# Two-layer metaformer on one core: GpSimd's operand tiles of layer 0 are placed at different offsets modulo 64 bytes, and three constants of layer 1 are made between the layers

## The chip, the cores and the metric

The kernel runs on 1 core of a Trainium2 chip. The metric is the device time of that core in microseconds (us). The time before is the median of three runs. The profile is one further execution, taken by the hardware profiler; its time is given beside them.

## The reference, cut to what matters

The input is `x` of 2 x 96 channels x 96 x 96. Each of two layers adds a mixer and then a quantized feed-forward network (FFN):

```python
x = x + conv0(ln(x));  x = x + ffn0(ln(x))      # layer 0: selective scan over windows
x = x + conv1(ln(x));  x = x + ffn1(ln(x))      # layer 1: attention with 5x5 depthwise taps
```

The core of layer 0's mixer, for four scan directions, 192 inner channels and 16 states, is

```python
dA = exp(dt[..., None] * A)
h  = h * dA + (dt * u)[..., None] * b
y  = einsum('bkdn,bkn->bkd', h, c)
```

Before it stand a projection, a 3x3 convolution that yields one offset pair per pixel, a bilinear sampling with these offsets, and the softplus that makes `dt`. After it stand a norm, a gate (`Y * zs`), a projection and the FFN.

## The kernel before, in words

**Layer 0.** The image is cut into 32 stripes of 6 rows (576 tokens, `T`), 16 to a batch element. For each stripe there are three parts.

- `_l0_front` prepares it. TensorE projects and convolves; `sample` interpolates bilinearly with seven GpSimd instructions for each half of the channels (lines 609 to 615: `dif`, `top`, `bot`, with `xin` and the fractions `fr`); `steps` makes the step sizes and inputs with four GpSimd instructions for each of six blocks (lines 743 to 746: `e`, `r`, `dl`, `du`, with `x1` or `x2`). `dl` and `du` go to DRAM by DMA (`store`) and come back spread over the partitions (`dlr`, `dur`).
- `_l0_scan` runs 64 units of 128 partitions x 3 x 288 elements. In a unit (`unit`), TensorE spreads `b` into the PSUM tile `bp` (`spread`, line 1040, two buffers), VectorE multiplies it with `dur` (`product`, line 1044), VectorE scans along time into an `h` tile (`scan`, line 1060, `P.nh` = 6 buffers), GpSimd multiplies `h` in place with `cre`, the spread `c` (`times_c`, line 1065, four `cre` buffers), and TensorE folds the states into `y` (`states`, line 1077). ScalarE makes the decays `dA` (`decay`, line 1025).
- `_l0_back` norms, gates on GpSimd (line 921: `Y`, `zs`), projects, and runs the FFN, whose last step is a GpSimd add of an fp32 and an fp16 tile (line 867).

**Order.** The three parts are not issued as written: each operation is handed to `_Plan` with an engine, a cost and a due time. `_Plan.order` lays all of layer 0 out on a model of the engines with a limited number of slots for each tag, and `_Plan.issue` emits the operations in the order of their planned starts; `_in_order` then pins that order on every engine and on the DMA queue of SyncE. The front of stripe n+1 and the back of stripe n-1 are so mixed between the units of stripe n. Each engine works strictly in its order.

**Placing.** Each slot becomes a tile of its own in a pool (`issue`: `t.pool.tile(...)`). All fp32 row tiles that GpSimd reads are multiples of 64 bytes long (576 x 4 = 2304 = 36 x 64; `h`: 864 x 4 = 3456 = 54 x 64), and in the built program they all start at a multiple of 64 bytes. Only `xin`, with rows of 98 elements read from the second column on, is entered at other offsets.

**Layer 1** (`_layer1`) follows: norm and projections (`_l1_before`), attention, and rows (`_l1_rows`). The constants `k.ones`, `k.join` and `k.onesb` are used there alone; `tile_metaformer` makes them ahead of layer 0, with two GpSimd memsets and two VectorE copies.

Of the kernel before, what the change touches and what calls it, by code (L numbers as in the profile page):

```python
# [1 line left out]

# [6 lines left out]
F32 = mybir.dt.float32  # L9
HP = mybir.dt.float16  # L10
BF = mybir.dt.bfloat16
# [14 lines left out]
C = 96  # L26
HW = 96
NTOK = HW * HW
WIN = 6
NW = HW // WIN  # L30
SEQ = WIN * WIN
T = WIN * HW
H2 = T // 2
# [4 lines left out]
NBL = C // CB  # L38
# [5 lines left out]
HEADS = 3  # L44
HD = 32
# [27 lines left out]
class _Tile:  # L73


    def __init__(self, plan, pool, tag, bufs, shape, dtype, name):
        self.pool, self.tag, self.shape, self.dtype, self.name = pool, tag, shape, dtype, name
        self.slots = plan.slots.setdefault((id(pool), tag), [[None, 0.0, ""] for _ in range(bufs)])
        self.queue = plan.queues.setdefault((id(pool), tag), [])
        self.slot, self.ap, self.users, self.writes, self.reads = None, None, [], [], []  # L80

    def place(self):

        if self.tag != "p" and self.queue[0] is not self:
            return None
        return min((s for s in self.slots if s[0] is None), key=lambda s: s[1], default=None)
# [15 lines left out]
class _Plan:  # L102
# [4 lines left out]
        self.k, self.ops, self.slots, self.queues = k, [], {}, {}  # L107
        self.rate = {}

    def tile(self, pool, shape, tag, bufs=1, dtype=F32, name=None):  # L110
        return _Tile(self, pool, tag, bufs, shape, dtype, name or tag)

    def held(self, ap, name):

# [98 lines left out]
    def issue(self):  # L213
        tab = None
        for o in self.order():
            for t in o.tiles:
                if t.ap is None:
                    n = [s is t.slot for s in t.slots].index(True)
                    t.ap = t.pool.tile(
                        t.shape, t.dtype, tag=f"{t.tag}{n}", name=t.name, bufs=1  # L220
                    )
            if o.tab is not None and o.tab != tab:
                tab = o.tab
                if tab == "e":
                    _exp_ln(self.k)
            o.run()


def _exp_ln(k):

    k.nc.scalar.add_instruction(
        mybir.InstLoadActFuncSet(
            name=k.nc.get_next_instruction_name(),
            engine=mybir.EngineType.Activation,
            act_func_set_id=EXP_LN,
            ins=[],
            outs=[],
        )
    )
# [205 lines left out]
def _l0_front(k, P, S, f, x, b, s, at):  # L445
# [3 lines left out]
    nc = k.nc  # L449
# [1 line left out]
    lo, hi = max(r0, 0), min(r0 + 8, HW)  # L451
    half2 = lambda v: v.rearrange("p (c n) -> p c n", c=2)
    n0 = len(S.ops)
    temp = lambda shape, name: S.tile(P.front, shape, "g", P.ng, name=name)
    ps = lambda name: S.tile(P.ps, [128, 512], "p", P.np, name=name)
    row = lambda name, bufs, dtype=F32: S.tile(P.front, [128, T], name, bufs, dtype)

    def pe(cols, run, r, w, also=()):
        S.op("pe", _cost("pe", cols), run, r, w, also=also)

    def act(cols, run, r, w, tab=None, times=1):
        S.op("act", times * _cost("act", cols), run, r, w, tab=tab)
# [4 lines left out]
    def pool(cols, run, r, w):  # L467
        S.op("pool", _cost("pool", cols), run, r, w)
# [55 lines left out]
            project(half, c)  # L524


    zs = f.zs = S.tile(P.hand, [C, 2, T], "zs", 2)

    def gate(half, c):
        pz = ps("pz")  # L530
# [13 lines left out]
    t = temp([C, 2, T], "t")  # L544
# [25 lines left out]

    fr = temp([C, 2, WIN, HW], "fr")

    def offset(yx, c):
        po = ps("po")
# [20 lines left out]

    xs0 = f.xs0 = S.tile(P.hand, [C, 2, T], "xs0", 2)
    xs1 = S.tile(P.front, [C, 2, T], "xs1", 1)
    dif, top, bot = temp([C, 2, 7, HW], "dif"), temp([C, 2, WIN, HW], "top"), temp([C, 2, WIN, HW], "bot")  # L600
    g = nc.gpsimd
    tt = g.tensor_tensor

# [42 lines left out]
    def order_of(o, xs):  # L646
# [48 lines left out]
            (rest,), (cd,))  # L695


        x1, x2 = row("x1", 1), row("x2", 1)

        block = lambda b: xs.ap[(b % NBL) * CB : (b % NBL) * CB + CB, b // NBL]  # L700

# [12 lines left out]
        def steps(m):  # L714


            bias = k.dt_b[:, o, m : m + 1]
            u = x2 if m == 2 else x1
            e, r, w, du = row("e", 2), row("r", 2), row("dl", 2), row("du", 2)
            for c in range(2):  # L720
                def half(c=c):
                    pt = ps("pt")
                    cols = slice(c * H2, (c + 1) * H2)
                    pe(H2, lambda: nc.tensor.matmul(  # L724
                        pt.ap[:, :H2], k.w_dt[:, o, m, :], xd.ap[:, cols],
                        start=True, stop=True), ((xd, c),), (pt,), (e, r))

                    def both():
                        nc.scalar.activation(e.ap[:, cols], pt.ap[:, :H2], AF.Abs, bias=bias)
                        nc.scalar.activation(r.ap[:, cols], pt.ap[:, :H2], AF.Relu, bias=bias)  # L730

                    act(H2, both, (pt,), ((e, c), (r, c)), times=2)

                half()

            def grow():
                nc.scalar.activation(e.ap, e.ap, AF.Exp, scale=-1.0)
                nc.scalar.activation(w.ap, e.ap, AF.Identity, bias=k.one)
                nc.scalar.activation(du.ap, w.ap, AF.Identity, bias=k.less)  # L739

            act(T, grow, (), (e, w, du), tab="e", times=3)
            act(T, lambda: nc.scalar.activation(w.ap, w.ap, AF.Ln), (), (w,), tab="e")
            pool(T, lambda: tt(e.ap, e.ap, du.ap, ALU.subtract), (du,), (e,))  # L743
            pool(T, lambda: tt(r.ap, r.ap, e.ap, ALU.add), (e,), (r,))
            pool(T, lambda: tt(w.ap, w.ap, r.ap, ALU.add), (r,), (w,))
            pool(T, lambda: tt(du.ap, w.ap, u.ap, ALU.mult), (w, u), (du,))  # L746


            def past():
                if m < 2:  # L750
                    g.memset(w.ap[:, (SEQ - 1 if m else 0) :: SEQ], PAST)
                else:
                    g.memset(w.ap[0:64, 0::SEQ], PAST)
                    g.memset(w.ap[64:128, SEQ - 1 :: SEQ], PAST)

            pool(16, past, (), (w,))

            def store(src, dst):
                def run():
                    if m < 2:  # L760
                        nc.sync.dma_start(dst[m].ap[:, 0:4, :], src.ap)
                    else:
                        for kk in range(2):
                            nc.sync.dma_start(
                                dst[kk].ap[:, 4:6, :], src.ap[64 * kk : 64 * kk + 64])

                S.op("sp", 1.0, run, (src,), [(d, m) for d in (dst if m == 2 else dst[m : m + 1])])

            d = [[v[o], v[o + 2]] for v in (f.dl, f.du)]
            store(w, d[0])  # L770
            store(du, d[1])

        for m in range(3):
            steps(m)
# [217 lines left out]
def _l0_section(k, P, S, f, first, o, h, kk, py, at, tau):  # L992


    nc = k.nc
# [12 lines left out]
    for name, d in (("dlr", f.dl[kg]), ("dur", f.du[kg])):  # L1008
        t = S.tile(P.rep, [128, NBL, T], name, 2)
# [24 lines left out]
    def unit(u, i, c, cre, dA, t0):  # L1034
        toks = slice(c * H2, (c + 1) * H2)
        bp = S.tile(P.ps, [128, 1024], "bp", 2)
        ht = S.tile(P.rep, [128, NBL, H2], "h", P.nh)

        def spread():
            nc.tensor.matmul(  # L1040
# [806 lines left out]
@with_exitstack  # L1847
def tile_metaformer(ctx: ExitStack, tc: tile.TileContext, a, out):
    nc = tc.nc
    k = Ctx()  # L1850
    k.nc = nc
    const = ctx.enter_context(tc.tile_pool(name="const", bufs=1))
    k.ident = const.tile([128, 128], F32, tag="ident", name="ident")
    make_identity(nc, k.ident)

    def filled(name, shape, v):
        t = const.tile(shape, F32, tag=name, name=name)
        nc.gpsimd.memset(t, v)
        return t

    k.kvq = [const.tile([C, C], F32, tag=n, name=n) for n in ("k_w", "v_w", "q_w")]
    k.mean96 = filled("mean96", [C, C], 1.0 / C)

    k.less_mean = const.tile([C, C], F32, tag="less_mean", name="less_mean")
    nc.vector.tensor_tensor(k.less_mean, k.ident[:C, :C], k.mean96, ALU.subtract)
    k.minus_mean192 = filled("minus_mean192", [C, C], -0.5 / C)
    k.less_mean192 = const.tile([C, C], F32, tag="less_mean192", name="less_mean192")
    nc.vector.tensor_tensor(k.less_mean192, k.ident[:C, :C], k.minus_mean192, ALU.add)
    k.mean192 = filled("mean192", [C, C], 1.0 / (2 * C))
    k.ones = filled("ones", [128, C], 1.0)  # L1870

    k.join = const.tile([128, C], F32, tag="join", name="join")
    nc.vector.tensor_copy(k.join, k.ident[:, :C])
    last = slice((HEADS - 1) * HD, HEADS * HD)
    nc.vector.tensor_copy(k.join[C:, last], k.ident[C:, C:])
    k.onesb = const.tile([128, 128], BF, tag="onesb", name="onesb")
    nc.gpsimd.memset(k.onesb, 1.0)
    k.eps6 = filled("eps6", [128, 1], EPS_LNC)
    k.eps5 = filled("eps5", [128, 1], EPS)
    k.one = filled("one", [128, 1], 1.0)  # L1880
    k.less = filled("less", [128, 1], -1.0)

    scratch = ctx.enter_context(tc.tile_pool(name="x2d", bufs=1, space=DRAM))
    x2d = scratch.tile([NB, C, NTOK], F32, tag="x2d", name="x2d")
    _layer0(k, tc, a, a["x"], x2d)
    _layer1(k, tc, a, x2d, out)


# [60 lines left out]
```

## Time and profile before

| | |
|---|---|
| median of 3 runs | 8538.53 us (8529.44 to 8542.1) |
| the profiled execution's own time | 8525.04 us |
| its span | 8523.3 us |
| TensorE matmul busy | 7295.1 us (86%) |
| VectorE busy | 7815.6 us (92%) |
| ScalarE busy | 6339.3 us (74%) |
| GpSimd busy | 6026.9 us (71%) |
| first and last scan (line 1060) start | 153.5 and 6472.0 us |

The times of single instructions come from the profiled execution. In a row of a group the columns are: line, engine, operation, output and inputs by tile name, shapes, count, then the busy time in us and the mean of one instruction in ns, and last the idle time of the engine just before them with what ended it. PE is TensorE, DVE is VectorE, ACT is ScalarE, POOL is GpSimd, SP is SyncE. In a timeline a row gives start and length in us; brackets at its end give the idle time before and who ended it. A busy time is no bound by itself: GpSimd is at 71% of the span only because layer 1, about a quarter of the span, hardly uses it.

### The profile page before, as it was taken

The page shows a single profiled execution, that of the slowest core. Times are in us where ns is not written, and L with a number is a line of the kernel's source. Part 1 is how long each engine was busy: PE and PEld are TensorE (multiplying, and loading weights), DVE is VectorE, ACT ScalarE, POOL GpSimd, SP SyncE. Part 2 cuts the span into 40 slices and gives each one's busy share as a digit, 9 for nine tenths or more (in the row PEclk, how much of TensorE's full clock was granted, in tenths as well). Part 3 has the DMA queues.
Part 4 walks back from the last instruction along what each step waited for, and adds up shares of the span by engine and source line. Part 5 has one row for each costly group of instructions (what it writes and reads, how often), then busy time and mean ns, then how long its engine had stood idle before and what let it go on. Part 6 is the DMA issues. An engine that isn't in the chain of part 4 may idle for free. (4 is left out here: it accounts for less than half of the span.)

```text
span 8523.3 us, 118902 instructions
## 1 busy us (share of the span) xinstructions
PE 7295.1 (86%) x43653; PEld 3402.1 (40%) x43653; DVE 7815.6 (92%) x5398; ACT 6339.3 (74%) x10688; POOL 6026.9 (71%) x3835
## 2 busy tenths in 40 slices
PE   7888888888888888888888888888866999989998
PEld 4443444444443444444444444443423223542245
DVE  3899999999999999999999999999996998959988
ACT  5777777777777777777777777777755886778867
POOL 4999999999999999999999999999984000110001
PEclk8899999999989888988999998989867999989999
DMA  2444444444444444444444444444442000110001
GB/s 89 141 153 148 150 152 147 148 151 144 149 146 144 151 146 152 149 150 153 146 150 151 146 145 151 146 151 150 146 143 76 3 2 14 34 48 3 2 21 32
DMA packets 339992, 985.62 MB, mean 116 GB/s; under 512 B 50152, under 2 KB 51872, under 8 KB 339104
## 3 DMA queue, kind: packets, MB, share of 16 engines
q1 hardware_dynamic: 337488, 977.74, 36.8%
q8 instruction: 347, 5.69, 0.3%
q14 instruction: 253, 2.07, 0.1%
q10 hardware_dynamic: 1904, 0.12, 0.0%
HBM read 797.19 MB, written 139.25 MB: 110 GB/s over the span
## 5 line engine op out<-in xcount | busy, mean ns | idle before, releaser
L1065 POOL TENSOR_TENSOR h<-h,cre 128x864 f32<-128x864 f32 x2048 | 4121.2, 2027 | 428.2 <-DVE h L1060 277.3
L1060 DVE TENSOR_TENSOR_SCAN h<-dA,bp 128x864 f32<-128x864 f32 x2048 | 3996.6, 1953 | 105.5 <-PE y L1077 25.5
L1025 ACT ACTIVATE dA<-dlr,A 128x576 f32<-128x576 f32 x3072 | 2155.9, 765 | 815.3 <-DVE h L1060 758.5
L1044 DVE TENSOR_TENSOR bp<-dur,bp 128x864 f32<-128x864 f32 x2048 | 2135.5, 1044 | 201.8 <-PE bp L1040 80.4
L1077 PE MATMUL y<-h,fold 128*32 128x288 f32 (+2 forms) x18432 | 1856.8, 449 | 465.3 <-POOL h L1065 444.4
L551 PE MATMUL pc<-xin,off 96*96 96x288 f32 x4608 | 1331.7, 421 | 0.1
L1077 PEld LDWEIGHTS y<-h,fold 128*32 128x32 f32 x18432 | 756.1, 117 | 1245.1 <-POOL h L1065 809.6
L1413 ACT ACTIVATE pr<-sc 128x960 f32<-128x960 f32 (+1 forms) x1080 | 954.1, 937 | 201.7 <-PE sc L1409 181.5
L1040 PE MATMUL bp<-bt,selb 128*128 128x288 bf16 x2048 | 640.9, 314 | 516.9 <-DVE h L1060 506.5
L1493 DVE TENSOR_TENSOR sums<-sums,pr 128x3840 f32<-128x3840 f32 (+1 forms) x240 | 959.0, 3996 | 56.7 <-ACT pr L1413 34.4
L1585 POOL MEMSET vch<- 96x32 f32 x16 | 2.4, 153 | 1298.1 <-DVE dist L1447 1208.1
L551 PEld LDWEIGHTS pc<-xin,off 96*96 96x96 f32 x4608 | 705.9, 165 | 505.9 <-issue 236.8
L1040 PEld LDWEIGHTS <-selb 128*128 128x128 bf16 x2048 | 201.5, 99 | 1204.1 <-DVE h L1060 930.4
L1409 PE MATMUL sc<-qH,kH 32*128 32x480 f32 (+1 forms) x3240 | 627.1, 602 | 10.1 <-DMA q<-qH 5.1
L1409 PE MATMUL sc<-q,kH 32*128 32x480 f32 (+1 forms) x1080 | 564.6, 602 | 0.0
L1475 PE MATMUL av<-pr,vT 128*32 128x480 f32 (+1 forms) x4320 | 533.2, 564 | 3.7 <-ACT av L1500 3.5
L1666 DVE SCALAR_TENSOR_TENSOR acc<-vch,lepe_w,acc 96x1152 f32<-96x1152 f32 x320 | 469.2, 1466 | 8.2 <-ACT vch L1601 0.4
L867 POOL TENSOR_TENSOR x<-x,fy 96x576 f32<-96x576 f32 x32 | 55.0, 1719 | 479.5 <-ACT fy L866 415.4
L1409 PEld LDWEIGHTS sc<-qH,kH 32*128 32x128 f32 x3240 | 218.9, 184 | 419.1 <-issue 219.9
L724 PE MATMUL pt<-xd,w_dt 96*128 96x288 f32 x768 | 290.5, 474 | 15.1 <-ACT xin L516 7.2
L743 POOL TENSOR_TENSOR e<-e,du 128x576 f32<-128x576 f32 x192 | 272.6, 1420 | 31.4 <-ACT du L739 30.9
L746 POOL TENSOR_TENSOR du<-dl,x 128x576 f32<-128x576 f32 x192 | 271.5, 1414 | 6.6
(270 smaller groups left out, 10018.1 us busy)
## 6 DMA issues: line engine op xcount, KB each, us to landing
cre<-c_d SPq DMA_DIRECT2D x1024, 288.0 KB
dur<-du_d SPq DMA_DIRECT2D x256, 864.0 KB
dlr<-dl_d SPq DMA_DIRECT2D x256, 864.0 KB
x<-xs SPq DMA_DIRECT2D x512, 72.0 KB
du_d<-du SPq DMA_DIRECT2D x128, 288.0 KB
dl_d<-dl SPq DMA_DIRECT2D x128, 288.0 KB
du_d<-du SPq DMA_DIRECT2D x128, 144.0 KB
dl_d<-dl SPq DMA_DIRECT2D x128, 144.0 KB
```

The costliest lines, as they stand in the source:

```text
L551: pe(H2, lambda: nc.tensor.matmul(pc.ap[:C, :H2], k.w_c1[:, ih, tap, oh * C : (oh + 1) * C], xin.ap[:, ih, 3 * c + dy : 3 * c + dy + 3, dx ...
L1025: nc.scalar.activation(dA.ap[:, :, blk, :], dlr.ap[:, blk, :].rearrange("p (c n) -> p c n", c=2), AF.Exp, scale=k.A[:, i, kg, h, blk : blk ...
L1040: nc.tensor.matmul(bp.ap[:, :H2], k.selb[:, kk, i, :], f.bc[o].ap[:, toks], start=True, stop=True)
L1044: nc.vector.tensor_tensor(bp.ap[:, : NBL * H2].rearrange("p (b n) -> p b n", b=NBL)[:, ::-1], dur.ap[:, ::-1, toks], bp.ap[:, :H2].unsquee ...
L1060: nc.vector.tensor_tensor_scan(hv, dv, bv, 0.0, ALU.mult, ALU.add)
L1065: nc.gpsimd.tensor_tensor(ht.ap, ht.ap, cre.ap[:, toks].unsqueeze(1).to_broadcast([128, NBL, H2]), ALU.mult)
L1077: nc.tensor.matmul(dst, k.fold, v, start=False, stop=stop)
L1409: nc.tensor.matmul(two[to // 2][:, to % 2, :n], kH[rows, k0 : k0 + 128], q, start=True, stop=True)
L1413: nc.scalar.activation(pr[:, 2 * i : 2 * i + 2, :n], two[i][:, :, :n], AF.Exp, scale=HD**-0.5)
L1475: nc.tensor.matmul((main if s < HEADS else other)[s * HD : (s + 1) * HD, :n], vT[:, blk, hd, :], pr[:, place(s, p), :n], start=at == 0, st ...
L1493: nc.vector.tensor_tensor(both, both, pr[:, :, :, :n], ALU.add)
L1666: S.op("dve", 1.43, lambda: nc.vector.scalar_tensor_tensor(acc.ap, src(), W.lw[:, t : t + 1], acc.ap, ALU.mult, ALU.add), (vch,), (acc,))
```

## The change

A tile may now be given a `skip`: its slot is allocated longer by `lead` elements (equal to `skip` unless given), and the tile begins `skip` elements (of 4 bytes) after the slot's start. The tiles of layer 0 that GpSimd reads in pairs get different skips. The lengths of slots change with that, so slots that follow can start elsewhere modulo 64 as well. No instruction of layer 0 is added, removed or changed in shape.

```diff
+def _place(t, tag):
+
+    if t.skip is None:
+        return t.pool.tile(t.shape, t.dtype, tag=tag, name=t.name, bufs=1)
+    n = math.prod(t.shape[1:])
+    flat = t.pool.tile([t.shape[0], n + t.lead], t.dtype, tag=tag, name=t.name, bufs=1)
+    v, d = flat[:, t.skip : t.skip + n], t.shape[1:]
...
-    zs = f.zs = S.tile(P.hand, [C, 2, T], "zs", 2)
+    zs = f.zs = S.tile(P.hand, [C, 2, T], "zs", 2, skip=12)
...
-    fr = temp([C, 2, WIN, HW], "fr")
+    fr = temp([C, 2, WIN, HW], "fr", 5)
...
-    dif, top, bot = temp([C, 2, 7, HW], "dif"), temp([C, 2, WIN, HW], "top"), temp([C, 2, WIN, HW], "bot")
+    dif, top, bot = temp([C, 2, 7, HW], "dif"), temp([C, 2, WIN, HW], "top", 2), temp([C, 2, WIN, HW], "bot")
...
-        x1, x2 = row("x1", 1), row("x2", 1)
+        x1, x2 = row("x1", 1, skip=14), row("x2", 1, skip=9)
...
-            e, r, w, du = row("e", 2), row("r", 2), row("dl", 2), row("du", 2)
+            e, du, r, w = (row(name, 2, skip=n) for name, n in (("e", 0), ("du", 1), ("r", 2), ("dl", 6)))
...
-        ht = S.tile(P.rep, [128, NBL, H2], "h", P.nh)
+        ht = S.tile(P.rep, [128, NBL, H2], "h", P.nh, skip=(2, 4, 8, 1)[i], lead=8)
```

The second part moves the three constants of layer 1 into a pool that is opened after `_layer0`; four small constants that layer 0 needs stay ahead of it.

```diff
-    k.ones = filled("ones", [128, C], 1.0)
...
     _layer0(k, tc, a, a["x"], x2d)
+    const = ctx.enter_context(tc.tile_pool(name="const1", bufs=1))
+    k.ones = const.tile([128, C], F32, tag="ones", name="ones")
+    nc.gpsimd.memset(k.ones, 1.0)
 
     k.join = const.tile([128, C], F32, tag="join", name="join")
     nc.vector.tensor_copy(k.join, k.ident[:, :C])
...
     nc.vector.tensor_copy(k.join[C:, last], k.ident[C:, C:])
     k.onesb = const.tile([128, 128], BF, tag="onesb", name="onesb")
     nc.gpsimd.memset(k.onesb, 1.0)
```

In the built programs the order of instructions on TensorE, ScalarE and SyncE is the same before and after. On GpSimd the two memsets alone change place. On VectorE the two copies into `join` move to between the layers, the second behind the first line of `band`, and a few short instructions of the weights' preparation change places with neighbours.

Modulo 64 bytes, the second operand then starts after the first by: `e`,`du` 4 or 36; `r`,`e` 56; `dl`,`r` 16 or 48; `dl`,`x1` 32; `dl`,`x2` 12; `dif`,`fr` 20; `bot`,`fr` 20; `bot`,`top` 8; `Y`,`zs` 48. An `h` slot is now 3488 bytes, which is 54 x 64 + 32, so `h` slots start at 0 and 32 in turn, and `h` and `cre` differ by 16, 24, 28, 32, 48, 56, 60 or 0, each for 256 of the 2048 units. Line 867 is left as it is.

More of the change, by code (lines that the diff above doesn't have):

```diff
@@ L1 @@
+import math
 from contextlib import ExitStack
@@ L80, in __init__ @@
         self.slot, self.ap, self.users, self.writes, self.reads = None, None, [], [], []
+        self.skip = None
     def place(self):
@@ L108, in __init__, with tile @@
         self.rate = {}
-    def tile(self, pool, shape, tag, bufs=1, dtype=F32, name=None):
-        return _Tile(self, pool, tag, bufs, shape, dtype, name or tag)
+    def tile(self, pool, shape, tag, bufs=1, dtype=F32, name=None, skip=None, lead=0):
+        t = _Tile(self, pool, tag, bufs, shape, dtype, name or tag)
+        t.skip, t.lead = skip, lead or skip
+        return t
     def held(self, ap, name):
@@ L218, in issue @@
                     n = [s is t.slot for s in t.slots].index(True)
-                    t.ap = t.pool.tile(
-                        t.shape, t.dtype, tag=f"{t.tag}{n}", name=t.name, bufs=1
-                    )
+                    t.ap = _place(t, f"{t.tag}{n}")
             if o.tab is not None and o.tab != tab:
@@ L226, in issue @@
             o.run()
+def _place(t, tag):
[4 more added lines that the diff above has]
+    v, d = flat[:, t.skip : t.skip + n], t.shape[1:]
+    names = [f"d{j}" for j in range(len(d))]
+    if len(d) == 1:
+        return v
+    return v.rearrange(f"p ({' '.join(names)}) -> p {' '.join(names)}", **dict(zip(names[1:], d[1:])))
 def _exp_ln(k):
@@ L453, in _l0_front @@
     n0 = len(S.ops)
-    temp = lambda shape, name: S.tile(P.front, shape, "g", P.ng, name=name)
+    temp = lambda shape, name, skip=0: S.tile(P.front, shape, "g", P.ng, name=name, skip=skip)
     ps = lambda name: S.tile(P.ps, [128, 512], "p", P.np, name=name)
-    row = lambda name, bufs, dtype=F32: S.tile(P.front, [128, T], name, bufs, dtype)
+    row = lambda name, bufs, dtype=F32, skip=None: S.tile(
+        P.front, [128, T], name, bufs, dtype, skip=skip)
     def pe(cols, run, r, w, also=()):
@@ L1869, in tile_metaformer @@
     k.mean192 = filled("mean192", [C, C], 1.0 / (2 * C))
-    k.ones = filled("ones", [128, C], 1.0)
[L1872 to L1877, printed above, removed]
     k.eps6 = filled("eps6", [128, 1], EPS_LNC)
@@ L1885, in tile_metaformer @@
     _layer0(k, tc, a, a["x"], x2d)
+    const = ctx.enter_context(tc.tile_pool(name="const1", bufs=1))
+    k.ones = const.tile([128, C], F32, tag="ones", name="ones")
+    nc.gpsimd.memset(k.ones, 1.0)
+    k.join = const.tile([128, C], F32, tag="join", name="join")
+    nc.vector.tensor_copy(k.join, k.ident[:, :C])
+    last = slice((HEADS - 1) * HD, HEADS * HD)
+    nc.vector.tensor_copy(k.join[C:, last], k.ident[C:, C:])
+    k.onesb = const.tile([128, 128], BF, tag="onesb", name="onesb")
+    nc.gpsimd.memset(k.onesb, 1.0)
     _layer1(k, tc, a, x2d, out)
```

## The prediction

> **What bounds the kernel now.** I read first the busy time in windows. From 3500 to 4500 us, deep in layer 0, the columns are TensorE, its weight loads, VectorE, ScalarE, GpSimd:
>
> ```profile
> 3500.00:4500.00 1000.00, 852.32 (x5046) 418.04 (x5045) 964.73 (x683) 770.45 (x1322) 934.06 (x576) 0.90 0.47 149
> ```
>
> VectorE is the bound, with 35 us in 1000 idle; GpSimd comes second, at 93%. The groups of instructions name the work:
>
> ```profile
> L1065 POOL TENSOR_TENSOR h<-h,cre 128x864 f32<-128x864 f32 x2048 | 4121.2, 2027 | 428.2 <-DVE h L1060 277.3
> L1060 DVE TENSOR_TENSOR_SCAN h<-dA,bp 128x864 f32<-128x864 f32 x2048 | 3996.6, 1953 | 105.5 <-PE y L1077 25.5
> L1044 DVE TENSOR_TENSOR bp<-dur,bp 128x864 f32<-128x864 f32 x2048 | 2135.5, 1044 | 201.8 <-PE bp L1040 80.4
> ```
>
> Undisturbed, VectorE repeats a unit every 2.945 us, as the timeline near the end of layer 0 shows:
>
> ```profile
> 6439.56 1.95 DVE L1060 TENSOR_TENSOR_SCAN h<-dA,bp 128x864 f32<-128x864 f32 x1
> 6441.42 1.04 DVE L1044 TENSOR_TENSOR bp<-dur,bp 128x864 f32<-128x864 f32 x1
> 6442.50 1.95 DVE L1060 TENSOR_TENSOR_SCAN h<-dA,bp 128x864 f32<-128x864 f32 x1
> ```
>
> A stripe's floor is 64 x 2.945 = 188.5 us, plus two each of line 508 (0.533), line 912 (0.732) and line 827 (0.431), 3.4 us: 191.9 us. From the first scan (153.5) to the last (6472.0) a stripe takes 6318.5 x 64 / 2047 = 197.5 us. So 5.6 us a stripe, about 180 us in all, are VectorE's waits: the most that quicker GpSimd work can return in mid-layer. The waits of VectorE from 200 to 6400 us say for whom (total, times, longest):
>
> ```profile
> DVE bp L1044 <- PE bp L1040: 80.4, 80, 3.3
> DVE bp L1044 <- PE y L1077: 48.9, 31, 3.1
> DVE h L1060 <- PE y L1077: 25.5, 12, 3.8
> DVE bp L1044 <- POOL h L1065: 9.9, 22, 0.8
> ```
>
> With two lesser POOL rows (3.7 and 2.7) that is 171 us. TensorE is named most, but it works in order, and the timeline of one stall shows it held up by GpSimd:
>
> ```profile
> 4196.69 1.20 PE L1077 MATMUL y<-h,fold 128*32 128x288 f32 x6 [1.99 <-POOL h L1065]
> 4198.16 5.97 POOL L1065 TENSOR_TENSOR h<-h,cre 128x864 f32<-128x864 f32 x3
> 4202.33 0.97 PE L1077 MATMUL y<-h,fold 128*32 128x216 f32 x12
> 4203.56 2.03 DVE L1044 TENSOR_TENSOR bp<-dur,bp 128x864 f32<-128x864 f32 x2 [3.33 <-PE bp L1040]
> ```
>
> GpSimd had run e, h, r, dl, h, du without a pause from 4188.4; TensorE lost 1.99 us on `h`, then had 4.3 us of the back's projection (lines 932 and 935, from 4198.0) ahead of the next `bp`. So about 60% of this stall (1.99 of 3.33) is GpSimd's and 40% is TensorE's own density.
>
> **What an offset costs on GpSimd.** The groups by form, GpSimd alone:
>
> ```profile
> L743 POOL TENSOR_TENSOR e<-e,du 128x576 f32<-128x576 f32 x192 | 272.6, 1420 | 31.4 <-ACT du L739 30.9 <-DVE bp L1044 0.4
> L613 POOL TENSOR_TENSOR bot<-bot,xin 96x576 f32<-96x576 f32 x64 | 83.6, 1306 | 2.8
> L609 POOL TENSOR_TENSOR dif<-xin 96x672 f32<-96x672 f32 x64 | 83.5, 1306 | 30.9 <-ACT xin L516 30.9
> L867 POOL TENSOR_TENSOR x<-xr,fy 96x576 f32<-96x576 f32 x32 | 40.8, 1276 | 18.2 <-ACT fy L866 18.2
> L1193 POOL TENSOR_TENSOR hs<-xn 96x288 f32<-96x288 f32 x32 | 21.2, 664 | 88.2 <-DVE xn L1171 88.2
> L1196 POOL TENSOR_TENSOR xs<-hs 96x144 f32<-96x144 f32 x32 | 15.6, 486 | 2.5
> ```
>
> Operands at equal offsets modulo 64 lie on one line: 144 elements 486 ns, 576 about 1416, 864 2027, that is 178 + 2.139 ns an element. The two groups whose operands are one element apart (lines 609 and 1193) lie on another: (1306 - 664) / (672 - 288) = 1.672 ns an element, 182 ns fixed. Line 613, at offsets that shift by 8 bytes a row from 20 to 60, lies between: (1306 - 180) / 576 = 1.955. Line 867 drifts through all offsets, fp32 against fp16: 1.90.
>
> **What the Trainium skill says.** (1) "GPSIMD Engine Reference", section "Elementwise — side-by-side cycle accounting", gives about 2.6 cycles an element for two inputs, which share one read port, and calls that the floor; the specifications say 1.2 GHz. The equal-offset line agrees (2.139 x 1.2 = 2.57); lines 609 and 1193, at 2.0, are below that floor, so here the measurement decides. (2) "SBUF — State Buffer", "Who interferes with whom": a VectorE instruction with at most one SBUF input doesn't contend with GpSimd. Product and scan each have one; the trace agrees, with scans at 1923 to 1956 ns throughout. A quicker GpSimd doesn't shorten VectorE's instructions. (3) The same page, "Operand start alignment", says that any multiple of the element size is legal, and that its runs timed nothing.[...]
>
> **The change part by part.**
> - `times_c`, 2048 instructions. Bounds: 182 + 864 x 1.672 = 1626 ns and 180 + 864 x 1.955 = 1869; 256 units keep equal offsets (2027). The new offsets are mostly like line 613's, but no row is quite like it, so I take the middle, 1748, for seven eighths: mean 1783, saving 244 ns. 64 x 0.244 = 15.6 us a stripe.
> - Lines 743 to 746, 24 a stripe: bounds 1145 and 1306, taken 1226 of 1416: 4.6 us. Lines 610, 612, 614 and 615, 8 a stripe at about 0.18: 1.4. Line 921, 2 at 0.19: 0.4. Lines 609, 611 and 613 stay apart and stay as they are.
> - Sum: GpSimd falls from 188 us a stripe (64 x 2.027 + 24 x 1.416 + 8 x 1.405 + 6 x 1.306 + 2 x 1.416 + 1.28 + memsets) to 166; 177 if all offsets are like line 613's, 154 if all are free. VectorE needs 191.9, so GpSimd's backlog after a burst of front work drains several times faster than now.
> - What VectorE gets: of the 171 us, 60% if the stall shown is typical (103), all if backlog was the root each time (in 172 of its 175 gaps over 0.15 us GpSimd had run for 6 us without a pause of 0.15 us, counted in the timeline). I take 70%: 120 us. Late next is TensorE's density.
> - The start: VectorE first waits 45.5 us for `dur`. On that path lie 8 cheaper instructions of `sample` (76.6 to 93.4 us, 1.4 us) and 8 to 12 of `steps` (114.4 to 136.0, 2 us, some under ScalarE's `du`): 3 us. After the last scan: one `h`, two `Y`: 0.6 us.
> - Other readers and writers of the moved tiles (ScalarE, TensorE, VectorE's scan, DMA): taken at nothing. TensorE's taps of line 551 read `xin` 0, 1 and 2 elements along and start 243 ns apart each; ScalarE's copies to `xin` (one element in) take a median 464 ns against 466 into aligned `axc`. Not shown is the scan's write: bounds 0 and 5% (98 ns), an estimate: three times the spread that line 1060 shows by itself, 1923 to 1956 ns. The moved DMAs (`x1`, `x2`, `dl`, `du`) ride in queues 47% busy and land ahead of need; only the first stripe's are on the path, at most 1 to 2 us. A gain there has no reason.
> - The constants: two memsets (0.18 and 0.20 us) and two copies (about 0.2 each, as line 339) leave a start where GpSimd next waits 31 us: nothing. Between the layers, GpSimd's stand before the `xs` memset (6510.75) and end well before its 10.6 us wait for `xn`; VectorE's stand in front of `band`, which waits for TensorE and ScalarE already, and 6.2 us of idle follow before `xn`. Without that cover: 0.4 us each. Layer 1's tiles move by 1024 bytes, so its offsets stay.
>
> Sum: 120 + 3 + 0.6 = 124 us. The profiled execution, 8525.0 with 1.7 us around its span, would be 8401; its median lies 13.5 us higher, so I forecast 8415.
>
> **Rivals.**
> - TensorE's density is most of the stalls. For it: TensorE is 85% busy, with 4.3 us of matmuls in a row. Against it: 404 us of TensorE's own waits are for `h`. A third of 171 us, and 3: 8538 - 60 = 8478.
> - The offset isn't what parts lines 609 and 1193 from the rest, and `h` stays near 2027: the change doesn't do what it says. Against it: three points on one line, two on the other. About 8535.
> - Slower: the scan, on the bounding engine, writes `h` off 64 bytes and lengthens. It decides from 124 / 2048 = 61 ns (3%) on; at 5% it costs 2048 x 98 ns = 200 us: 8415 + 200 = 8615. Against it: line 1447 writes `dist` one element in, at 630 ns for 480 elements, no more an element than line 1651's 544 for 384.
>
> **How the numbers follow.** Forecast (8350 to 8465) 0.70, density 0.15, no effect 0.08, slower scan 0.07. The low end is all 180 us and the start's; the high end takes in the density case. Faster by over 0.2% (17 us, what a measurement here can tell from no change) 0.85, within it 0.08, slower 0.07.
>
> **What would show it.** Line 1065 between 1626 and 1869 ns, in up to eight steps, one near 2027; lines 743 to 746 at 1145 to 1306; 609, 613 and 867 unchanged; 1060 and 1044 within 10 ns; GpSimd near 83% in mid-layer, VectorE near 98%; TensorE's wait for `h` a fraction of 404 us. A scan over 2015 ns, or waits of VectorE that stay at 171 us, would make me wrong.

## The result, and the profile after

The changed kernel takes 8444.31 us (median of 4 runs, 8443.66 to 8449.37), against 8537.53 us (median of 4) for the kernel before: a ratio of 0.9893, with a 95% interval of 0.9881 to 0.9906. That is 93 us less; 124 were forecast. Lines have moved by 16: the product is now line 1060, the scan 1076, `times_c` 1081, the fold 1093, the spread 1056, and the four lines of `steps` 759 to 762.

The time came from where it was looked for:

| profiled execution | before | after |
|---|---|---|
| its own time (span) | 8525.0 (8523.3) | 8449.4 (8447.6) |
| start to first scan | 153.5 | 152.1 |
| first scan to last scan | 6318.5 | 6237.6 |
| of that over VectorE's floor (6132) | 186 | 105 |
| last scan to end | 2051.3 | 2057.9 |
| GpSimd a stripe (sum of its durations in layer 0, over 32) | 188.5 | 179.1 |

VectorE's floor between the two scans is worked out from the profile of before: 2047 units of 2.945 us, and 103.9 us of the three lines of the front and the back (508, 912 and 827) that fall in between.

Now the window of the changed kernel in mid-layer (columns as before: TensorE, weight loads, VectorE, ScalarE, GpSimd):

```profile
3500.00:4500.00 1000.00, 855.82 (x5102) 418.47 (x5106) 975.31 (x693) 779.04 (x1346) 907.21 (x589) 0.91 0.48 152
```

VectorE rose from 96.5% to 97.5%; GpSimd fell only from 93.4% to 90.7%. Its groups by form tell why:

```profile
L1081 POOL TENSOR_TENSOR h<-h,cre 128x864 f32<-128x864 f32 x2048 | 3965.5, 1947 | 616.1 <-DVE h L1076 357.4 <-PE pc L567 141.6 <-PE y L1093 40.1
L762 POOL TENSOR_TENSOR du<-dl,x 128x576 f32<-128x576 f32 x192 | 271.7, 1415 | 6.6
L761 POOL TENSOR_TENSOR dl<-dl,r 128x576 f32<-128x576 f32 x192 | 270.9, 1411 | 9.1 <-ACT dl L758 4.1
L760 POOL TENSOR_TENSOR r<-r,e 128x576 f32<-128x576 f32 x192 | 231.9, 1208 | 3.3
L759 POOL TENSOR_TENSOR e<-e,du 128x576 f32<-128x576 f32 x192 | 231.1, 1204 | 33.3 <-ACT du L755 33.2
L937 POOL TENSOR_TENSOR Y<-Y,zs 96x576 f32<-96x576 f32 x64 | 89.9, 1405 | 12.5 <-DVE Y L928 12.5
L629 POOL TENSOR_TENSOR bot<-bot,xin 96x576 f32<-96x576 f32 x64 | 83.5, 1305 | 2.8
L631 POOL TENSOR_TENSOR bot<-bot,fr 96x576 f32<-96x576 f32 x64 | 76.9, 1202 | 1.4
```

All these pairs now differ modulo 64, but for an eighth of `h`, and yet lines 761, 762 and 937 took what equal offsets took, while others fell by 200 ns. Within line 1081 there are only two speeds: 512 instructions took up to 1757 ns, the others 1994 or more. Its instructions, sorted by the addresses of the two tiles in the built program (second operand's start minus the first's, bytes modulo 64; 256 units each), have these means:

| difference | 0 | 16 | 24 | 28 | 32 | 48 | 56 | 60 |
|---|---|---|---|---|---|---|---|---|
| modulo 16 | 0 | 0 | 8 | 12 | 0 | 0 | 8 | 12 |
| ns | 2028 | 2025 | 1714 | 2024 | 2024 | 2021 | 1715 | 2023 |

The other pairs whose rows are plain (one run of elements, without `xin`) fit the same rule: fast at 4 or 8 modulo 16 (`e`,`du` 4 and 36; `r`,`e` 56; `fr` 20; `bot`,`top` 8), slow at 0 or 12 (`dl`,`r` 16 and 48; `dl`,`x1` 32; `dl`,`x2` 12; `Y`,`zs` 48). That is the theory tested below. The rival is that a pair need only differ modulo 64. (In the built program of before, the tiles of these pairs all start at 32 modulo 64, not at a multiple of 64 as said above. Their differences are 0 all the same.)

VectorE's waits in the changed kernel, 150 to 6400 us:

```profile
DVE bp L1060 <- PE bp L1056: 51.1, 53, 2.2
DVE bp L1060 <- PE y L1093: 28.8, 19, 3.6
DVE h L1076 <- PE y L1093: 27.2, 16, 3.6
DVE h L1076 <- POOL h L1081: 2.4, 1, 2.4
```

The first two rows fell from 129 to 80; the third didn't fall (27.2 us, before 25.5). TensorE's wait for `h` fell from 404 us to about 150. First the row of before, then two of the changed kernel, all from 200 to 6400 us:

```profile
PE y L1077 <- POOL h L1065: 404.1, 455, 3.5
```
```profile
PE bp L1056 <- DVE h L1076: 679.6, 737, 3.2
PE y L1093 <- POOL h L1081: 152.0, 156, 2.7
```

### The profile page after: what moved, and what is told of

It is laid out like the page before. It is cut to its first block, busy times and chain, and to the rows that moved or that the text cites. A ratio compares the mean times of both kernels' runs of the same rounds, so it can differ in the third digit from the quotient of the medians.

```text
span 8447.6 us, 118902 instructions
## 1 busy us (share of the span) xinstructions
PE 7320.6 (87%) x43653; PEld 3406.4 (40%) x43653; DVE 7806.9 (92%) x5398; ACT 6339.6 (75%) x10688; POOL 5742.1 (68%) x3835
## 5 line engine op out<-in xcount | busy, mean ns | idle before, releaser
L1081 POOL TENSOR_TENSOR h<-h,cre 128x864 f32<-128x864 f32 x2048 | 3965.5, 1947 | 616.1 <-DVE h L1076 357.4
L1076 DVE TENSOR_TENSOR_SCAN h<-dA,bp 128x864 f32<-128x864 f32 x2048 | 3996.8, 1953 | 105.4 <-PE y L1093 27.2
L1060 DVE TENSOR_TENSOR bp<-dur,bp 128x864 f32<-128x864 f32 x2048 | 2133.6, 1043 | 132.9 <-PE bp L1056 51.1
L761 POOL TENSOR_TENSOR dl<-dl,r 128x576 f32<-128x576 f32 x192 | 270.9, 1411 | 9.1 <-ACT dl L758 4.1
L762 POOL TENSOR_TENSOR du<-dl,x 128x576 f32<-128x576 f32 x192 | 271.7, 1415 | 6.6
```

The source lines that it names most:

```text
L1060: nc.vector.tensor_tensor(bp.ap[:, : NBL * H2].rearrange("p (b n) -> p b n", b=NBL)[:, ::-1], dur.ap[:, ::-1, toks], bp.ap[:, :H2].unsquee ...
L1076: nc.vector.tensor_tensor_scan(hv, dv, bv, 0.0, ALU.mult, ALU.add)
L1081: nc.gpsimd.tensor_tensor(ht.ap, ht.ap, cre.ap[:, toks].unsqueeze(1).to_broadcast([128, NBL, H2]), ALU.mult)
```

## The experiments

"Mid-layer waits" are the time from first to last scan less 6132 us, in the profiled execution of each run. The kernel before was timed again in each of the three rounds of experiments, with medians of 8528.6, 8531.7 and 8532.4 us. The ratios are to the kernel before of the same round, so kernels of different rounds are compared by ratio.

**Which offset is fast?** Three kernels are the changed one with another `h` line.

```diff
-        ... skip=(2, 4, 8, 1)[i], lead=8)
+        ... skip=2, lead=8)      # e1_h_skip2
+        ... skip=4, lead=8)      # e2_h_skip4
+        ... skip=3, lead=8)      # e3_h_skip3
```

Expected of the first: 

> Every h tile begins 2 elements (8 bytes) into its slot, whatever the quarter; slots still start at 0 and 32 in turn, so cre lies 56 or 24 bytes after h modulo 64. In the changed kernel the units at 56 and 24 took 1715 ns and those at 0, 16, 28, 32, 48 and 60 took 2021 to 2028. Theory (the second operand's start minus the first's, modulo 16 bytes: 4 or 8 is fast, 0 or 12 slow): all 2048 units near 1715. GpSimd then needs 64 x 0.23 = 15 us less a stripe than in the changed kernel, 165 us against VectorE's 192. If VectorE's waits are GpSimd's backlog, most of the 100 us left in mid-layer go: about 8380 to 8400. If TensorE's density holds them, 8420 to 8440.

Of the second: 

> Every h tile begins 4 elements (16 bytes) into its slot: cre lies 48 or 16 bytes after h modulo 64, never 0. If it is enough to differ modulo 64 (as the change has it), h takes clearly less than 2027 ns and the time is at or below the changed kernel's 8444. Theory (modulo 16): every unit stays near 2024, and the time goes back up, to about 8490 to 8520, as the front's cheaper instructions are all that remains.

Of the third: 

> Every h tile begins 3 elements (12 bytes) into its slot: cre lies 52 or 20 bytes after h modulo 64, 4 modulo 16. Theory (4 or 8 modulo 16 is fast): all units near 1715, time as with 2 elements. Rival (only a distance of half a 16-byte line helps h, and the mirror images 4 and 12 are alike): all units near 2024, since 12 is slow in the changed kernel (units at 28 and 60).

The row of `times_c` among GpSimd's groups, first 2, then 4, then 3 elements:

```profile
L1081 POOL TENSOR_TENSOR h<-h,cre 128x864 f32<-128x864 f32 x2048 | 3494.9, 1713 | 1057.7 <-DVE h L1076 624.7 <-PE pc L567 175.6 <-PE y L1093 103.6
```
```profile
L1081 POOL TENSOR_TENSOR h<-h,cre 128x864 f32<-128x864 f32 x2048 | 4121.0, 2024 | 499.7 <-DVE h L1076 269.3 <-PE pc L567 148.7 <-PE y L1093 21.8
```
```profile
L1081 POOL TENSOR_TENSOR h<-h,cre 128x864 f32<-128x864 f32 x2048 | 3494.8, 1713 | 1067.1 <-DVE h L1076 625.1 <-PE pc L567 168.6 <-PE y L1093 112.7
```

With 4 elements every `h` and `cre` differ modulo 64 and none is faster: the rival falls. Times: 8445.75 (ratio 0.9899, 0.9884 to 0.9914), 8472.15 (0.9934, 0.992 to 0.9948) and 8442.93 (0.9898, 0.9883 to 0.9913). The times that had been expected of the first failed: 15 us a stripe less on GpSimd than in the changed kernel returned nothing (0.9899 against 0.9893), though TensorE's wait for `h` fell further, from 152 to 97 us. In the second, `h` is as slow as before, so its 56 us came from the front and `zs`, more than the theory had given them (8490 to 8520).

**Does the sign count?** Every `h` begins 1 element in, and the operands of `times_c` are named in the other order.

```diff
-        ht = ... skip=(2, 4, 8, 1)[i], lead=8)
+        ht = ... skip=1, lead=8)
-                ht.ap, ht.ap, cre.ap[:, toks]...to_broadcast([128, NBL, H2]), ALU.mult)
+                ht.ap, cre.ap[:, toks]...to_broadcast([128, NBL, H2]), ht.ap, ALU.mult)
```

Expected: 

> As the changed kernel, but every h tile begins 1 element in and the product names cre first and h second, so the second operand starts 4 (modulo 16) after the first, where the order h, cre would give 12, slow in the changed kernel (2023 ns). Theory (the sign counts: second minus first, 4 or 8 fast): all units near 1715. Rival (the tile that is written in place decides, or where the tile lies in its line): near 2024.

```profile
L1081 POOL TENSOR_TENSOR h<-cre,h 128x864 f32<-128x864 f32 x2048 | 3498.0, 1715 | 1053.2 <-DVE h L1076 615.4 <-PE pc L567 169.9 <-PE y L1093 104.3
```

With `h` one element in, the order `h`, `cre` had given 2023 in the changed kernel (12 modulo 16 and its like, 28 and 60); the order `cre`, `h` gives 1715. Tiles one element apart are slow when the second operand starts 4 bytes before the first (12 modulo 16) and fast when it starts 4 after. This kernel was run once: 8438.31 us.

**Where does the gain come from?** Each part alone.

```diff
-        ht = ... skip=(2, 4, 8, 1)[i], lead=8)      # e6_front_only: h as before
+        ht = S.tile(P.rep, [128, NBL, H2], "h", P.nh)
```

e7_h_only keeps this line of the changed kernel and drops all other skips; e5_consts_only drops every skip and keeps the move of the constants.

Expected of the constants alone: 

> The three constants of layer 1 are made between the layers; every tile of layer 0 starts where it did before. Theory: they lie beside other work on both sides, so the time is that of the kernel before within 0.1%, about 8530. Rival: layer 1 begins later by them (the profile of the changed kernel has 6.6 us more after the last scan): 8535 to 8540, with the 6.6 us in the same place.

Of the front and `zs` alone: 

> As the changed kernel, but the h tiles start where they did before (same offset as cre modulo 64): every h unit near 2026 ns. Theory (modulo 16): it equals the kernel with h 4 elements in, 8472, since that gave h no gain either; so about 56 us of the 93 come from 20 cheaper short instructions a stripe, 4 us a stripe. Rival (the h units carry most of the gain): 8500 or more.

Of `h` alone: 

> As the changed kernel in h alone; the front's tiles and zs start where they did before. A quarter of the h units near 1715 ns, 5 us a stripe less of GpSimd. If stalls come from bursts of front work between h units, less than half of the gain: 8490 to 8510. If all GpSimd time counts alike, 5 of the 9 us a stripe saved and so about 8480.

| kernel | GpSimd a stripe, us | mid-layer waits | time | ratio to before |
|---|---|---|---|---|
| before | 188.5 | 186 | 8531.7 | |
| constants alone | 188.3 | 186 | 8532.2 | 1.0002 (0.9993 to 1.001) |
| `h` alone | 183.1 | 138 | 8490.9 | 0.996 (0.9944 to 0.9975) |
| front and `zs` alone | 184.1 | 135 | 8472.9 | 0.9938 (0.9923 to 0.9953) |
| the change | 179.1 | 105 | 8444.3 | 0.9893 (0.9881 to 0.9906) |
| `h` at 2 elements | 164.1 | 102 | 8445.8 | 0.9899 (0.9884 to 0.9914) |

The row of the change is the result above (kernel before: 8537.5 us); that of `h` at 2 elements is of the round with 8528.6. The constants cost nothing that the timed runs can tell. The front part saves 4.4 us of GpSimd a stripe and returns 59 us; `h` saves 5.4 and returns 41. The theory for the front part (8472) came true, and so did the first figure for `h` alone (8490 to 8510). But that a microsecond saved in the middle of a burst is worth more isn't shown: the two intervals overlap, and in the profiles the mid-layer waits fell almost alike, by 51 and 48 us. The front part alone, at 8472.9, equals the kernel with `h` 4 elements in, at 0.9938 and 0.9934: to move `h` without making GpSimd faster returns nothing. After 9 us a stripe the curve is flat.

**All pairs near.** The fix by the rule found:

```diff
-    zs = ... skip=12)
+    zs = ... skip=2)
-        x1, x2 = row("x1", 1, skip=14), row("x2", 1, skip=9)
+        x1, x2 = row("x1", 1, skip=1), row("x2", 1, skip=1)
-            ... (("e", 0), ("du", 1), ("r", 2), ("dl", 6)))
+            ... (("e", 0), ("du", 1), ("r", 2), ("dl", 0)))
-        ht = ... skip=(2, 4, 8, 1)[i], lead=8)
+        ht = ... skip=2, lead=8)
```

Expected: 

> All pairs of layer 0 that GpSimd reads, but those with xin, get 4 or 8 modulo 16: h 2 elements in, dl 0, x1 and x2 1, zs 2, the rest as in the changed kernel. Theory: lines of dl, du and Y fall from 1405 to 1415 to about 1205, h to 1715; GpSimd needs about 161 us a stripe. Against the kernel with h at 2 alone that is 5 us a stripe less: another 5 to 25 us if backlog still costs VectorE, nothing if TensorE's density is all that is left. 8370 to 8400 by the first, 8420 by the second.

```profile
L762 POOL TENSOR_TENSOR du<-dl,x 128x576 f32<-128x576 f32 x192 | 231.5, 1206 | 6.6
L761 POOL TENSOR_TENSOR dl<-dl,r 128x576 f32<-128x576 f32 x192 | 231.2, 1204 | 10.9 <-ACT dl L758 6.4
L937 POOL TENSOR_TENSOR Y<-Y,zs 96x576 f32<-96x576 f32 x64 | 76.8, 1201 | 10.9 <-DVE Y L928 10.9
```

The three slow lines fell as the rule has it; GpSimd needs 161.2 us a stripe. The time is 8437.09 us (0.9891, 0.9875 to 0.9906), the best of the kernels that compute everything, though its interval doesn't part it from the change, and it is above both times expected. The mid-layer waits stay at 98 us. What holds them? Its timeline shows one of the stalls that recur every second stripe:

```profile
4889.29 1.27 PE L948 MATMUL pp<-xr,ident 96*96 96x288 f32 x2 [0.92 <-ACT r L746]
4890.36 2.13 PE L951 MATMUL pp<-zs,w_outb 96*96 96x288 f32 x4
4891.13 5.06 POOL L1081 TENSOR_TENSOR h<-h,cre 128x864 f32<-128x864 f32 x3
4892.28 1.91 PE L951 MATMUL pp<-Y,out_proj 96*96 96x288 f32 x4
4894.03 0.29 PE L1056 MATMUL bp<-bt,selb 128*128 128x288 bf16 x1
4894.35 1.06 DVE L1060 TENSOR_TENSOR bp<-dur,bp 128x864 f32<-128x864 f32 x1 [1.71 <-PE bp L1056]
```

VectorE waits for `bp`, which stands behind 4.7 us of the back's projection, one operation to the plan, where a unit lasts 2.945 us. No wait for `h` is in it. The block had itself begun late, after 0.92 us in which TensorE waited for ScalarE (`r`, line 746). The next such stall, 20 us on, has no such wait ahead of its block and is longer:

```profile
4907.98 1.28 PE L948 MATMUL pp<-xr,ident 96*96 96x288 f32 x2
4914.41 2.03 DVE L1060 TENSOR_TENSOR bp<-dur,bp 128x864 f32<-128x864 f32 x2 [2.28 <-PE bp L1056]
```

**Is it TensorE's load?** Part of the convolution is left out of the kernel with all pairs near, so this one doesn't compute the whole:

```diff
-            pe(H2, lambda: nc.tensor.matmul(
+            pe(H2, lambda: None if ih and tap < 8 else nc.tensor.matmul(
```

Expected: 

> The kernel with all pairs at 4 or 8 modulo 16, with 8 of the 18 matmuls of each convolution left out (the second half's first 8 taps); the order of all else is kept. TensorE has 2048 fewer matmuls, some 500 us. Theory (TensorE's density between two bp matmuls holds VectorE now): the 97 us of VectorE's waits in mid-layer fall to under 40, and the time to 8360 to 8385. Rival (what is left is ScalarE, GpSimd bursts or the buffers of h and bp): waits stay over 75 us and the time at 8425 to 8437.

VectorE's waits from 150 to 6400 us:

```profile
DVE bp L1060 <- PE bp L1056: 57.2, 61, 4.3
DVE bp L1060 <- PE y L1093: 21.4, 25, 3.3
DVE h L1076 <- PE y L1093: 19.3, 14, 3.5
```

The time is 8430.70 us (0.9884, 0.9869 to 0.9899), and the mid-layer waits are 105. The theory, as put, fell, and the rival's figures came. The small gain isn't mid-layer's: the first scan starts at 129.6 us instead of 151.3. But the relief was smaller than expected. In the windows of mid-layer the granted clock was 0.85 to 0.87 (the third figure from the end), against 0.89 to 0.92, and a matmul of the convolution took 482 ns instead of 422, so that TensorE's busy share fell from 86% to 81% only. Without and then with these matmuls left out:

```profile
3500.00:4500.00 1000.00, 859.56 (x5115) 421.69 (x5115) 973.86 (x691) 780.64 (x1347) 817.34 (x587) 0.90 0.48 151
L567 PE MATMUL pc<-xin,off 96*96 96x288 f32 x4608 | 1335.3, 422 | 1.5 <-ACT xin L532 1.5
```
```profile
3500.00:4500.00 1000.00, 808.42 (x4794) 385.77 (x4794) 975.59 (x691) 788.38 (x1360) 822.22 (x593) 0.86 0.48 152
L567 PE MATMUL pc<-xin,off 96*96 96x288 f32 x2560 | 892.5, 482 | 1.7 <-ACT xin L532 1.4
```

So this much less load returned nothing in mid-layer. What a lighter TensorE at an unchanged clock would return isn't shown.

**Is it the block?** In the kernel with all pairs near, the two products with `zs` are left out of the projection:

```diff
-                for h in range(2):
+                for h in range(2 * n):
```

Expected: 

> The kernel with all pairs at 4 or 8 modulo 16; of the five products in a row of the back's projection (one block on TensorE of 5.3 us in its timeline, with a bp matmul behind it) the two with zs are left out, which leaves 3.2 us; order kept. Leaving out 592 us of convolution moved the time by 7 us only, but those matmuls stand singly between others. Theory (the length of a block that TensorE can't break, not its load, holds VectorE): the stalls of 1.7 and 2.3 us a pair of stripes go, VectorE's waits fall by 30 to 60 us, time 8380 to 8405. Rival (the h and bp buffers, or ScalarE): no change, 8430 to 8437.

(The 592 us in it were an estimate, 8/18 of the convolution; in the two rows above TensorE's busy time falls by 443.) The time is 8422.78 us (0.987, 0.9854 to 0.9887). That is 14 us below the kernel with all pairs near, or 18 by the ratios, whose intervals still overlap. The mid-layer waits are 82. VectorE's waits from 150 to 6400 us:

```profile
DVE bp L1060 <- PE y L1093: 38.5, 22, 3.2
DVE bp L1060 <- PE bp L1056: 19.9, 27, 4.1
DVE h L1076 <- PE y L1093: 19.4, 14, 3.5
```

With all pairs near these rows were 17.1, 50.7 and 19.3. The waits for `bp` behind the block went, as the theory has it, but most of them came back as waits named after `y`. The mid-layer waits fell by 16 us, about half of the least expected (30), and the time lies between the theory's and the rival's figures: a cause among several. The edit takes work off TensorE as well as shortening the block; that a larger relief, of the convolution, returned nothing in mid-layer speaks for the length.

**Splitting the block.** The projection is handed to the plan as five operations of one product each, nothing left out, in the kernel with all pairs near and in the kernel before:

```diff
-        op("pe", 5 * H2, run, (Y, zs, (x1, c)), (pp,))
+        op("pe", H2, lambda: nc.tensor.matmul(...), (Y, zs, (x1, c)), (pp,))
+        def part(n, w, v, h):
+            op("pe", H2, lambda: nc.tensor.matmul(...), (v,), (pp,))
...      # part is called once for each of the other four products
```

Expected with all pairs near: 

> The kernel with all pairs at 4 or 8 modulo 16; the back's projection is handed to the plan as five operations of one product each, so that the plan may put a bp matmul between them; nothing is left out. The plan's whole order changes with it. Theory (block length): at least the 4 us a pair of stripes of those stalls go, 8375 to 8405. Rival: other orders bring other stalls, 8425 to 8445.

Expected of the kernel before: 

> The kernel before, with the projection as five operations; offsets as before. If the block is a cause by itself (40% of the stall read in the profile of before), it gains alone: 8490 to 8515. If GpSimd's backlog stands behind nearly all of VectorE's waits before, under 10 us: 8520 to 8535.

Both were slower than what they were made from, and outside all figures expected: 8532.74 us (0.9999, 0.999 to 1.0008) and 8606.36 us (1.0085, 1.0068 to 1.0101). The whole order of layer 0 moves with the edit. In the first, products waited only 17.6 us for `bp` itself (200 to 6300 us), but scans waited 78.4 us and products 48.7 us for `y`, and the norm (`Y`) 43.7 us. So these two don't decide whether the block is a cause, and show how much the order counts: a different plan cost about as much as the whole change brought. With all pairs near, the offsets are worth 74 us under the new order too.

## Why the prediction was right, and where its sizes were off

**The mechanism held.** VectorE bounds layer 0, waits for TensorE, and TensorE waited for GpSimd; product and scan kept their durations (1043 and 1953 ns), and all of the gain lies between the first scan and the last. Of the signs that the prediction named, TensorE's wait for `h` fell to a fraction and VectorE came near 98% (97.5%); but line 1081 lay outside its bounds, and GpSimd stayed at 90.7% where 83% was forecast.

**`times_c`: mis-sized.** The step took 1783 ns as the mean, with 1626 and 1869 as bounds. Fast units take 1714, but only a quarter are fast, and the mean is 1947. The failed reading is that of line 613, taken as an intermediate speed for "far" offsets. Its rows move by 8 bytes, so its differences alternate between 4 and 12 modulo 16: half fast, half slow. (1204 + 1416) / 2 = 1310, against the 1306 in the row. So a mean over rows of two speeds was read as a third speed; that is argued from this sum, as no run moved `xin` alone.

**Lines 743 to 746, the sampling, `Y`: right for six lines of nine.** For lines 743 to 746, 1226 was taken; `e` and `r` came to 1206, `dl` and `du` stayed at 1411 to 1415, the four of the sampling came to 1202 and `Y` stayed at 1405. GpSimd fell by 9.4 us a stripe, not 22.

**What VectorE gets: 70% of 171 us: too much for any relief.** The change returned 81 us in mid-layer; with GpSimd 27 us a stripe lighter it would be 88. So about half was recoverable in this order, below the 60% that the one stall in the timeline had given; the raise to 70% rested on GpSimd having run without a pause before nearly every gap, which doesn't show that the gap was its doing. Both errors, of the relief and of its return, made the forecast too low. That less than half of the relief cost so little is luck: the first 9 us a stripe bring nearly all there is. With 4.4 us alone, the time was 8473, outside the range forecast.

**Late next: TensorE by the names of the waits.** The lighter load that was tried returned nothing in mid-layer. The block in the projection is one cause, worth 14 to 18 us here. What holds the other 80 us or so is open; the waits are named after `y` and `bp`, and the plan's order is the likely place, argued and not shown. The traces do say where they lie: with all pairs near, the stretches of 64 scans show 32 of the 98 us in five stripes (the first two, the two at the change of the batch element, and the last but one), and in the second batch element the others mostly alternate between 5.1 and 0.6 us.

**Start and end: not told apart from the spread.** The start took 1.4 us less, where 3 were forecast. But the six kernels with this front give first scans from 147.1 to 152.1 us, against 152.8 to 153.5 in the three with the front and the order as before: 1 to 6 us, with the 3 among them. After the last scan the profile has 6.6 us more, in layer 1. The profile with the constants alone has that too (2057.9), yet its timed runs are at 1.0002; the interval reaches to 8 us. The twelve kernels with the constants moved take 2054.4 to 2061.6 us after the last scan, the two others 2051.3 and 2049.6, so a few microseconds may be theirs. The shift arises at the first rows of layer 1 (`distT`, `vch`), where the kernel before with a split projection also came 9 us late and made most of it good. Whether the constants have a part in it isn't settled; the timed runs show no cost.

**Other readers and writers: right.** The scans of the changed kernel write from twelve different starts modulo 64, and their means by start are all 1951 to 1954 ns; the slower rival fell. Of the rivals, TensorE's density named the right engine for what remains, but with too little gain (60 us); "no effect" fell with lines 759 and 760.

## What to carry to other kernels

Before moving tiles apart by just any distance, sort the instructions by the difference of their operands' start addresses: a mean over a group can hide two speeds, and a group with shifting rows may be a mixture, not a point between. When the helper of the bounding engine gets faster, the gain is not its saved time but the stalls it caused; here the first 9 us a stripe returned 81 us of mid-layer waits and the next 18 returned 7.

## What the runs showed of the hardware that was not expected

- GpSimd's two-input fp32 instruction on plain rows has two speeds: about 184 ns + 1.77 ns an element (1204 at 576, 1714 at 864) where the second operand starts 4 or 8 bytes after the first modulo 16, and about 178 + 2.14 (486 at 144, 2027 at 864) where it is 0 or 12. These are straight lines through two points each. All differences tried fit: 0, 12, 16, 28, 32, 48 and 60 slow, 4, 8, 20, 24, 36, 40, 52 and 56 fast. The order of the operands decides between 4 and 12.
- Two groups don't fit: lines 609 and 1193, whose two operands are views of the same tile one element apart, lie at 1.67 ns an element, faster yet, and line 609 does so at 12 modulo 16, against the rule. Line 609 reads rows of 96 out of 98, line 1193 every second element. What sets them apart wasn't tried.
- With 8 of 18 matmuls of each convolution left out (line 567 fell from 1335 to 892 us, not to 10/18 = 742), the granted clock of TensorE fell from 0.91 to 0.86 (means of five windows in mid-layer).
